# Two mixture-of-experts layers cut into runs of four token tiles in place of eight, each run with its own slots, buffers and conditional part

## The chip, the core and the metric

The kernel runs on one core of a Trainium2 chip. A core has five engines that each take instructions in order from a queue of their own: TensorE (PE, with the loading of its weights shown apart as PEld), VectorE (DVE), ScalarE (ACT), GpSimd (POOL) and SyncE (SP), which here only starts transfers. Sixteen DMA engines move data between the chip's memory (HBM) and the core's on-chip memory. The metric is the time of one execution in microseconds (us) on the device. Beside the times there is a trace of one profiled execution.

## The reference

The input x is 2 batches of 1024 tokens with 256 features, in 32-bit floats. Six steps add to it:

```python
x = x + 0.5 * L0_ffn(layernorm(x))      # 8 experts, each token goes to 2, hidden size 176
x = x + rwkv(layernorm(x))              # time mixing and channel mixing along each batch
x = x + 0.5 * L0_ffn(layernorm(x))
x = x + 0.5 * L1_ffn(layernorm(x))      # 32 experts, each token goes to 6, hidden size 96
x = x + L1_attn(layernorm(x))
x = x + 0.5 * L1_ffn(layernorm(x))
```

Only the last three are touched here. A layer of the second kind is

```python
scores = sigmoid(x @ gate_w)
topk_w, topk_i = top_k(scores, 6)
topk_w = topk_w / (sum(topk_w) + 1e-20)
combine = sum(one_hot(topk_i, 32) * topk_w[..., None], axis=1)
act = silu(einsum('td,edf->tef', x, wg)) * einsum('td,edf->tef', x, wu)
routed = einsum('tef,efd,te->td', act, wd, combine)
shared = silu(x @ sg) * (x @ su) @ sd
return routed + shared
```

The attention between the two is linear and sums over a whole batch: with Q, K and V from one product, `A = sum(feature_map(rope(K)) * V)` over the 1024 tokens of the batch, and the result is `(A * rope(Q)) @ W_out + b_out`, added to its input. So a batch can't leave the attention before all of its tokens have come through the first L1 mixture, while the two batches don't depend on each other.

## The kernel before, in words

x stays on the chip as 16 tiles of 128 tokens by 256 features. Tiles 0 to 7 are the first batch (called half A), 8 to 15 the second (half B). Four tiles are a group (`BT` is 4).

**A mixture** (`sparse_moe`, from line 400) computes only the experts that a token has chosen. Its parts are functions that a program outside of them calls piece by piece:

- `prep` normalizes a group's four tiles, transposes them and computes the router's scores; `plan` turns the choices into slot numbers, such that the tokens of one expert lie together and every expert starts at a multiple of 128.
- `scatter` (line 560) writes each token's row to the memory tile `xs`, once per chosen expert, at its slot: 24 indirect DMA calls on POOL for four tiles with six choices. Calls come in threes, with five short POOL memsets behind each three as a pause.
- `owners` works out which expert owns each block of 128 slots (the tile `who`) and how many blocks are in use (`used`). `weights` looks up the weight of each choice, on DVE.
- `blocks` (line 877) goes through the blocks. Each is fetched from `xs` by SP (`fetch`), transposed on PE (`features`, tile px), multiplied by its expert's gate and up matrices (`inner`, tile pg, with the expert's number in a PE register that `look_up` loads four at a time), gated on ACT and DVE, transposed again (`turn`, tile ph), multiplied by the down matrix (`outward`, tile py), copied by DVE to a tile yb and stored by SP to the memory tile `ys`. `step` issues one stage each of five neighbouring blocks, so they overlap.
- `shared` computes the shared expert of tiles; `combine` fetches each token's rows back from `ys` (24 indirect DMA calls on POOL, line 801, eight buffers yk) and adds them to x with their weights on DVE (line 813).

How many blocks are needed depends on the choices. Eight tiles with six choices and 32 experts can need up to 79 blocks (`moe_blocks`, each expert rounded up to a multiple of 128). The first 68 (`SURE`) are always computed. The other 11 stand in a conditional part: `tc.If(n > sure)` around `rest()` (line 906), where PE, DVE, ACT and SP each compare the count, loaded from `used` at block 16, and jump over the part where it is not needed. Blocks between the count in use and 68 hold zeros: `fill_slots` writes zeros to all of `xs`, and to the rows of `ys` that only the conditional part would write, ahead of the layers.

**The halves.** In each pass of an L1 mixture half A is a run of 68 blocks, then half B is one. The tiles are called L1_0A and L1_0B in the first pass, and L1_1A and L1_1B in the second. A half's first group of tokens may be gathered once 55 blocks are stored (a count that its four tiles can't exceed), the second group once all are.

**The order of the work** is written down when the program is built. The main program calls the blocks, and a planner (`clock`) with estimated durations (1.41 us for an L1 block, 4.8 us for a shared tile, 1.27 us for an indirect call, 1.4 us for a pause) lets other threads put in their instructions when they are due: scatters, gathers, the attention of a half with the preparation of its second mixture (`second_pass`). `settle` holds the main program until something is planned. On the chip each engine follows this order, and waits are for data and buffers alone. The main program before, in its last part: shared experts of 0A; blocks 0A with the attention's first steps due behind them; blocks 0B, with attention of A, its second preparation and 0B's shared tiles put between; then `settle(lambda: 1 in ready2[0])`, `shared_of(m2[0])` (all eight shared tiles of 1A) and `settle(lambda: 1 in sent2[0])`; blocks 1A; blocks 1B with its shared tiles as `part`; and behind them the gathers of 1B. From 0B's blocks to 1A's blocks no run is under way; the attention of batch B lies there.

The functions that the change touches, as they are before it:

## Time and profile before

| | |
|---|---|
| median of 8 runs | 1457.09 us (1455.04 to 1461.97) |
| the profiled execution | 1457.8 us, of which the trace's span is 1456.0 us |
| mean granted TensorE clock | 0.896 of full speed |
| PE busy | 1265.4 us, 87% of the span |
| weight loads (PEld) | 970.5 us, 67% |
| DVE busy | 736.0 us, 51% |
| POOL busy | 666.4 us, 46% |
| ACT busy | 622.8 us, 43% |
| moved by DMA | 214.94 MB, a mean of 148 GB/s |
| instructions | 23152 |

A busy time is the sum of an engine's instructions over the span, so PE's 87% is a mean over stages that differ. The L1 part takes the second half: the first L1 gate product is at 735.8 us, 0A's blocks run to about 850, 0B's to 1053, 1A's from 1168 to 1280, 1B's to 1397, and the program ends at 1456. In rows of groups the form is line, engine, operation, output<-input by the program's names, and the count behind an x; tiles of the second half of the first pass have 0B in their name. The granted clock tells how fast PE was let run: at 0.5 a product takes twice its time.

### The profile page before, as it was taken

To read this page: it belongs to the slowest core of one execution; us is meant where nothing else is said; L and a number is where in the kernel's file an instruction comes from. 1 tells how busy PE (TensorE), PEld (TensorE's weight loads), DVE (VectorE), ACT (ScalarE), POOL (GpSimd) and SP (SyncE) were. 2 spreads that over 40 slices of the span, in tenths; PEclk is the share of its full clock that TensorE was granted. 3 is DMA by queue.
4 is the path that set the end of the run, shared out by engine and by line. 5 is a ranking of instruction groups with operands and counts; after the bars stand their busy time and mean duration, and the time that the engine had idled before them with its cause. 6 is when DMAs were issued, how large, how long until landed. Compare 5 with 4: busy or idle time off the path is not lost. (4 is left out here: it accounts for less than half of the span.)

```text
span 1456.0 us, 23152 instructions
## 1 busy us (share of the span) xinstructions
PE 1265.4 (87%) x6100; PEld 970.5 (67%) x6100; DVE 736.0 (51%) x2507; ACT 622.8 (43%) x1671; POOL 666.4 (46%) x1346
## 2 busy tenths in 40 slices
PE   6699889889999789999889988988888789989970
PEld 4577657455666767766668977767655678978850
DVE  5333545855642432456354446764687354455553
ACT  4023553477664123442434545443323244544520
POOL 1630522001110640467777255505667777166465
PEclk9589889889999679989969999997789699999995
DMA  9723422980002723433757776533322267677743
GB/s 284 231 78 104 137 77 89 310 298 1 0 0 64 197 80 101 138 102 113 216 166 241 214 204 198 161 106 97 110 59 76 80 196 244 201 230 238 233 125 105
DMA packets 195170, 214.94 MB, mean 148 GB/s; under 512 B 40892, under 2 KB 178012, under 8 KB 195036
## 3 DMA queue, kind: packets, MB, share of 16 engines
q1 hardware_dynamic: 170460, 146.22, 32.6%
q0 software_dynamic: 24576, 67.14, 15.1%
q8 instruction: 59, 0.97, 0.3%
q14 instruction: 75, 0.61, 0.2%
HBM read 103.04 MB, written 110.23 MB: 146 GB/s over the span
## 5 line engine op out<-in xcount | busy, mean ns | idle before, releaser
L801 POOL DMA_INDIRECT yk_L<-ys_L,idx_L x64 | 62.1, 970 | 186.9 <-DMA ys_L<-yb_L 124.5
L333 POOL MEMSET still<- 128x96 f32 x628 | 112.5, 179 | 35.9
L764 PE MATMUL pg_L_b<-L0gu,xbT_L 128*128 x312 | 110.5, 479 | 0.0
L566 POOL DMA_INDIRECT xs_L<-xn_L,idx_L x64 | 61.9, 967 | 74.5 <-DVE idx_L L557 37.0
L659 PE MATMUL pg_L<-L0sgu,xTs_L 128*128 128x352 f32 x256 | 89.6, 484 | 2.9 <-DVE h_L L650 2.9
L801 POOL DMA_INDIRECT yk_L_0B<-ys_B,idx_L_0B x48 | 48.9, 1019 | 74.8 <-DMA ys_B<-yb_L_0B 46.8
L781 PE MATMUL py_L_b<-L0down,hT_L_b 88*128 x312 | 82.0, 385 | 0.0
L801 POOL DMA_INDIRECT yk_L_0A<-ys_A,idx_L_0A x48 | 46.3, 964 | 70.1 <-DMA ys_A<-yb_L_0A 31.9
L801 POOL DMA_INDIRECT yk_L_1A<-ys_A,idx_L_1A x48 | 46.1, 961 | 60.5 <-DMA xb_L_1A<-xs_A 29.1
L781 PEld LDWEIGHTS py_L_b<-L0down,hT_L_b 88*128 88x128 f32 x312 | 59.7, 194 | 20.0 <-issue 1.0
L764 PEld LDWEIGHTS pg_L_b<-L0gu,xbT_L 128*128 128x128 f32 x312 | 56.5, 198 | 20.1 <-issue 3.0
L650 DVE TENSOR_TENSOR h_L_b<-g_L_b,pg_L_b 128x176 f32<-128x176 f32 x78 | 26.2, 336 | 83.2 <-ACT g_L_b L649 73.4
L983 PE MATMUL pkk_cm<-mk_cm,w_WkeyT 128*128 128x512 f32 x128 | 62.7, 622 | 5.2 <-DVE mk_cm L975 3.5
L659 PEld LDWEIGHTS pg_L<-L0sgu,xTs_L 128*128 128x128 f32 x256 | 47.9, 199 | 25.6 <-DVE h_L L650 4.6
L764 PE MATMUL pg_L_0B_b<-L1gu,xbT_L_0B 128*128 x272 | 59.9, 346 | 1.2 <-DVEq L906 1.0
L764 PE MATMUL pg_L_0A_b<-L1gu,xbT_L_0A 128*128 x272 | 59.5, 344 | 1.6 <-ACT g_L_0A_b L649 0.7
L801 POOL DMA_INDIRECT yk_L_1B<-ys_B,idx_L_1B x48 | 45.7, 951 | 31.3 <-DMA xb_L_1B<-xs_B 13.4
L764 PE MATMUL pg_L_1B_b<-L1gu,xbT_L_1B 128*128 x272 | 56.5, 330 | 2.8 <-issue 1.3
L995 PE MATMUL pkv_cm<-w_WvalT,sk_cm 128*128 128x256 f32 x256 | 58.0, 379 | 0.1
L764 PE MATMUL pg_L_1A_b<-L1gu,xbT_L_1A 128*128 x272 | 57.6, 335 | 0.3 <-DVE m_L_1B L193 0.2
L995 PEld LDWEIGHTS pkv_cm<-w_WvalT,sk_cm 128*128 128x128 f32 x256 | 48.3, 190 | 12.0 <-issue 5.0
L649 ACT ACTIVATE g_L_b<-pg_L_b 128x176 f32<-128x176 f32 x78 | 24.7, 317 | 73.2 <-PE pg_L_b L764 61.5
(639 smaller groups left out, 3394.0 us busy)
## 6 DMA issues: line engine op xcount, KB each, us to landing
xs_A<-zero SPq DMA_DIRECT2D x1, 10112.0 KB
xs_B<-zero SPq DMA_DIRECT2D x1, 10112.0 KB
xb_L<-xs_L SPq DMA_DIRECT2D x78, 128.0 KB
ys_L<-yb_L SPq DMA_DIRECT2D x78, 128.0 KB
xb_L_0A<-xs_A SPq DMA_DIRECT2D x68, 128.0 KB
ys_A<-yb_L_0A SPq DMA_DIRECT2D x68, 128.0 KB
xb_L_0B<-xs_B SPq DMA_DIRECT2D x68, 128.0 KB
ys_B<-yb_L_0B SPq DMA_DIRECT2D x68, 128.0 KB
```

The costliest lines, as they stand in the source:

```text
L333: d = nc.gpsimd.memset(still, 0.0)
L566: d = nc.gpsimd.indirect_dma_start(out=xs, out_offset=bass.IndirectOffsetOnAxis(ap=idx[:, t, k : k + 1], axis=0), in_=sent[g][t - BT * g], ...
L649: nc.scalar.activation(g, pg[:, 0:width], AF.Silu)
L650: nc.vector.tensor_tensor(dst, g, pg[:, width : 2 * width], ALU.mult)
L659: nc.tensor.matmul(pg, xbT[:, c, i * P : (i + 1) * P], w["sgu"][:, c, u, :, :].rearrange("p z w -> p (z w)"), start=(c == 0), stop=(c == D ...
L764: nc.tensor.matmul(pg, xbT[:, c, :], w["gu"][:, c, bass.ds(e, 1), :, :].rearrange("p e z h -> p (e z h)"), start=(c == 0), stop=(c == DC - 1),
L781: mm = nc.tensor.matmul(py, hT[0:HP, k, :], w["down"][:, bass.ds(e, 1), k, :].rearrange("p e d -> p (e d)"), start=(k == 0), stop=(k == C ...
L801: d = nc.gpsimd.indirect_dma_start(out=yk, out_offset=None, in_=ys[0 : n * P, :], in_offset=bass.IndirectOffsetOnAxis(ap=idx[:, t, k : k + ...
L983: nc.tensor.matmul(ps, w[:, c, oc * P : (oc + 1) * P], src[:, c, :], start=(c == 0), stop=(c == DC - 1),)
L995: nc.tensor.matmul(ps, src[:, c, i * P : (i + 1) * P], w[:, c, :], start=(c == 0), stop=(c == n - 1),)
```

## The change

The L1 mixtures are cut by groups of four tiles. In each pass there are four runs instead of two, called 0A0, 0A1, 0B0, 0B1 and 1A0, 1A1, 1B0, 1B1. Each has

- its own memory tiles `xs[q]` and `ys[q]`, q from 0 to 3, of 55 blocks each instead of 79 for each half (the second pass uses the first one's again);
- 34 blocks that are always computed and 21 in a conditional part of its own, so that eight conditional parts stand in the program instead of four;
- its own plan, owners and weights; `who` and `used` have five buffers, `idx` and `wk` six. A mixture no longer has a second group, so all of its gathers wait for its conditional part.

The program around it follows: the first pass sends a group's tokens as soon as that group is planned; `run_of` puts the next run's first steps behind the last blocks of one, where the next one's scatters are planned by then. The attention of half A is due from 0A0 on, that of half B from 0B0's end on. In the first pass the shared tiles of half A stand ahead of 0A0 and those of half B beside and behind 0B1. In the second pass a run's shared tiles are put in a list (`left`) that `spare` deals from; `sent_or_fill` uses it where the main program would wait until a run's scatters are planned, and what is left over stands behind 1B1's blocks. The count of a run is loaded at its block 16, as before.

```diff
-SURE = {"L0": moe_blocks(MOE["L0"]), "L1": 68}
+SURE = {"L0": moe_blocks(MOE["L0"]), "L1": 34}
...
-    def sparse_moe(layer, w, name, x, xs, ys, moe, given=None, out=None, bufs=2):
+    def sparse_moe(layer, w, name, x, xs, ys, moe, given=None, at=0, out=None, bufs=2):
...
+        ahead = 5 if layer == "L1" else bufs
-        idx = back.tile([P, NT, K], I32, tag="idx", name=f"idx_{name}", bufs=3)
-        wk = back.tile([P, NT, K], F32, tag="wk", name=f"wk_{name}", bufs=2)
-        who = moe.tile([1, P], I32, tag="who", name=f"who_{name}", bufs=bufs)
-        used = moe.tile([1, 1], I32, tag="used", name=f"used_{name}", bufs=bufs)
+        idx = back.tile([P, NT, K], I32, tag="idx", name=f"idx_{name}", bufs=6)
+        wk = back.tile([P, NT, K], F32, tag="wk", name=f"wk_{name}", bufs=6)
+        who = moe.tile([1, P], I32, tag="who", name=f"who_{name}", bufs=ahead)
+        used = moe.tile([1, 1], I32, tag="used", name=f"used_{name}", bufs=ahead)
...
-            n = min(WHO, (sure if b < sure else NBLK) - b)
+            n = min(WHO - b % WHO, (sure if b < sure else NBLK) - b)
...
-    for k, layer, tiles in (("L0", "L0", NT), ("A", "L1", HT), ("B", "L1", HT)):
+    for k, layer, tiles in (("L0", "L0", NT), *((q, "L1", BT) for q in range(NB))):
...
-        for h in range(2):
-            fill_slots(xs["AB"[h]], moe_blocks(MOE["L1"], HT), behind=m["latest"]["add"])
+        for q in range(NB):
+            fill_slots(xs[q], moe_blocks(MOE["L1"], BT), behind=m["latest"]["add"])
             fill_slots(
-                ys["AB"[h]][SURE["L1"] * P :, :],
-                moe_blocks(MOE["L1"], HT) - SURE["L1"],
+                ys[q][SURE["L1"] * P :, :],
+                moe_blocks(MOE["L1"], BT) - SURE["L1"],
                 behind=m["latest"]["add"],
             )
...
+    def rows_of(m, qs, added, rank=0):
+        for g, q in enumerate(qs):
+            yield from wait(lambda: q in m and 0 in m[q]["ready"])
+            yield clock.now + 3.0
+            yield from m[q]["combine"](0, rank)
+            added.add(g)
...
+    def run_of(m, q, sent, part=None):
+
+        def beside():
+            if q + 1 < NB and q + 1 in sent:
+                return m[q + 1]
+            return pieces_of(part) if part is not None else None
+
+        all_of(m[q]["blocks"](beside))
...
-    shared_of(m1[0])
-    settle(lambda: 1 in sent1[0])
-    filled()
+    all_of(parts(m1[0], m1[1]))
+    settle(lambda: 0 in sent1)
     clock.begin(1, second_pass(0))
-    clock.begin(1, sends(m2, ready2, sent2, 0, 1))
-    all_of(m1[0]["blocks"](lambda: m1[1] if 1 in sent1[1] else None))
-    settle(lambda: 1 in sent1[1])
-    clock.begin(3, second_pass(1))
-    clock.begin(2, sends(m2, ready2, sent2, 1, 2))
-    part = m1[1]["shared"](0, HT)
-    all_of(m1[1]["blocks"](lambda: pieces_of(part)))
+    clock.begin(1, sends(m2, range(QS), ready2, sent2, 1))
+    for q in range(NB - 1):
+        run_of(m1, q, sent1)
+        settle(lambda: q + 1 in sent1)
+        if q == QS - 1:
+            clock.begin(3, second_pass(1))
+            clock.begin(2, sends(m2, range(QS, NB), ready2, sent2, 2))
+    part = parts(*(m1[q] for q in range(QS, NB)))
+    run_of(m1, NB - 1, sent1, part)
     all_of(part)
     summed.add(1)
-    settle(lambda: 1 in ready2[0])
-    shared_of(m2[0])
-    settle(lambda: 1 in sent2[0])
-    filled()
+
     done = [set(), set()]
-    clock.begin(4, given_rows(m2[0], range(2), done[0], 4))
-    all_of(m2[0]["blocks"](lambda: m2[1] if 1 in sent2[1] else None))
-    settle(lambda: 1 in sent2[1])
-
-    clock.begin(5, given_rows(m2[1], range(2), done[1], 5))
-    part = m2[1]["shared"](0, HT)
-    all_of(m2[1]["blocks"](lambda: pieces_of(part)))
+    for h in range(2):
+        clock.begin(4 + h, rows_of(m2, range(QS * h, QS * h + QS), done[h], 4 + h))
+    left = []
+
+    def spare():
+        while True:
+            us = None
+            while left and us is None:
+                us = next(left[0], None)
+                if us is None:
+                    left.pop(0)
+            yield us
+
+    part = spare()
+
+    def sent_or_fill(q):
+        while q not in sent2:
+            us = next(part)
+            clock.run(1.0 if us is None else us)
+
+    for q in range(NB):
+        while q not in ready2:
+            clock.run(1.0)
+        left.append(m2[q]["shared"](0, BT))
+        sent_or_fill(q)
+        run_of(m2, q, sent2, part)
     pauses["on"] = False
-    all_of(part)
+    all_of(iter(lambda: next(part), None))
     settle(lambda: 1 in done[0], lambda: 1 in done[1])
```

More of the change, by code (lines that the diff above doesn't have):

```diff
@@ L426, in places @@
         def places(t):
-            h, i = divmod(t, HT)
+            h, i = divmod(t + at, HT)
             if h not in xn:
@@ L622, in weights @@
         def weights(h):
-            ts = slice(HT * h, HT * h + HT)
+            n = min(HT, NT)
+            ts = slice(n * h, n * h + n)
             for k in range(K):
                 same = moe.tile(
-                    [P, HT, E], F32, tag="same", name=f"same_{name}_{h}_{k}", bufs=1
+                    [P, n, E], F32, tag="same", name=f"same_{name}_{h}_{k}", bufs=1
                 )
@@ L631, in weights @@
                     slot[:, ts, :],
-                    top[:, ts, k : k + 1].to_broadcast([P, HT, E]),
+                    top[:, ts, k : k + 1].to_broadcast([P, n, E]),
                     ALU.is_equal,
@@ L1392, in macaron_kernel, with quad_moe @@
     summed0 = {0}
-    added0, summed, ready1, ready2 = set(), {0}, [set(), set()], [set(), set()]
-    sent1, sent2 = [set(), set()], [set(), set()]
-    def half(n, h, **more):
-        k = "AB"[h]
-        return sparse_moe(
-            "L1", w1, f"L1_{n}{k}", x[HT * h : HT * h + HT], xs[k], ys[k], moe_pool, **more
+    added0, summed = set(), {0}
+    ready1, ready2, sent1, sent2 = set(), set(), set(), set()
+    QS = NB // 2
+    places_of = {}
+    def quad_moe(n, q, given, **more):
+        h, g = divmod(q, QS)
+        return sparse_moe(
+            "L1",
+            w1,
+            f"L1_{n}{'AB'[h]}{g}",
+            x[BT * q : BT * q + BT],
+            xs[q],
+            ys[q],
+            moe_pool,
+            given=given,
+            at=BT * g,
+            **more,
@@ L1400, in half, with onward @@
         )
-    def onward(m, g, planned):
+    def onward(m, q, planned):
         with behind_blocks():
-            m["prep"](g)
+            m["prep"](0)
         yield clock.spent(6.0, 12.0)
-        if g == 0:
-            yield from wait(lambda: not planning)
-            planning.append(m)
+        yield from wait(lambda: not planning)
+        planning.append(m)
         with behind_blocks():
-            m["plan"](g)
-        yield clock.spent(3.5, 7.0)
-        planned.add(g)
-        if g == m["groups"] - 1:
-            planning.pop()
@@ L1418, in first_pass @@
-    def first_pass(h):
-        for g in range(2):
-            yield from wait(lambda: 2 * h + g in added0)
-            if g == 0:
-                yield from wait(lambda: h in summed0)
-                m1[h] = half(0, h)
-            yield from onward(m1[h], g, ready1[h])
-        with behind_blocks():
-            m1[h]["owners"]()
-            m1[h]["weights"](0)
-        yield clock.now
+            m["plan"](0)
+        yield clock.spent(2.5, 5.0)
+        planned.add(q)
+        planning.pop()
@@ new lines, in onward @@
+        with behind_blocks():
+            m["owners"]()
+            m["weights"](0)
+        yield clock.now
+    def first_pass(h):
+        for q in range(QS * h, QS * h + QS):
+            yield from wait(lambda: q in added0 and h in summed0)
+            if q % QS == 0:
+                places_of[h] = (
+                    moe_pool.tile([P, HT, D], F32, tag="xn", name=f"xn_{h}", bufs=2),
+                    moe_pool.tile([P, DC, SEQ], F32, tag="xT", name=f"xTs_{h}", bufs=2),
+                )
+            m1[q] = quad_moe(0, q, places_of[h])
+            yield from onward(m1[q], q, ready1)
@@ L1431, in second_pass @@
     def second_pass(h):
         added, result = set(), {}
-        clock.begin(0, given_rows(m1[h], range(2), added))
+        qs = range(QS * h, QS * h + QS)
+        clock.begin(0, rows_of(m1, qs, added))
         yield from wait(lambda: h in summed)
         yield from attend(h, moe_pool, added, result)
-        m2[h] = half(
-            1,
-            h,
-            given=result["given"],
-            out=out[HT * h * P : (HT * h + HT) * P, :],
-        )
-        for g in range(2):
+        for q in qs:
+            m2[q] = quad_moe(
+                1, q, result["given"], out=out[BT * q * P : (BT * q + BT) * P, :]
+            )
@@ L1445, in second_pass @@
             with behind_blocks():
-                for t in range(BT * g, BT * g + BT):
+                for t in range(BT * (q % QS), BT * (q % QS) + BT):
                     result["out_of"](t)
             yield clock.spent(7.0, 8.0)
-            yield from onward(m2[h], g, ready2[h])
-        with behind_blocks():
-            m2[h]["owners"]()
-            m2[h]["weights"](0)
-        yield clock.now
-    def sends(m, planned, sent, h, rank):
-        for g in range(2):
-            yield from wait(lambda: g in planned[h])
-            yield from m[h]["scatter"](g, rank)
-            sent[h].add(g)
+            yield from onward(m2[q], q, ready2)
@@ L1462, in between, with sends @@
+    def rows_of(m, qs, added, rank=0):
[4 more added lines that the diff above has]
+            added.add(g)
+    def sends(m, qs, planned, sent, rank):
+        for q in qs:
+            yield from wait(lambda: q in planned)
+            yield from m[q]["scatter"](0, rank)
+            sent.add(q)
     def between():
         yield from given_rows(m0, (0, 1), added0)
-        yield from wait(lambda: 0 in ready1[0])
@@ L1465, in between @@
-        yield from m1[0]["scatter"](0)
+        yield from sends(m1, (0,), ready1, sent1, 0)
         yield from given_rows(m0, (2,), added0)
-        yield from wait(lambda: 1 in ready1[0])
-        yield from m1[0]["scatter"](1)
-        sent1[0].add(1)
+        yield from sends(m1, (1,), ready1, sent1, 0)
         yield from given_rows(m0, (3,), added0)
-        for g in range(2):
-            yield from wait(lambda: g in ready1[1])
-            yield from m1[1]["scatter"](g)
-        sent1[1].add(1)
+        yield from sends(m1, (2, 3), ready1, sent1, 0)
@@ L1476, in macaron_kernel, with parts @@
+    def run_of(m, q, sent, part=None):
[4 more added lines that the diff above has]
+        all_of(m[q]["blocks"](beside))
+    def parts(*ms):
+        for m in ms:
+            yield from m["shared"](0, BT)
     clock.begin(0, between())
@@ L1481, in macaron_kernel @@
     summed0.add(1)
-    settle(lambda: 1 in ready1[0])
+    settle(lambda: 1 in ready1)
     l0_stack.close()
```

## The prediction

> **What bounds the kernel now.** I read the stretches first (busy time of each engine between landmarks), then the rows of the block tiles, the engines' order of time around a conditional part, and last the gathers that end the program. In the stretches the columns after the length are busy us of PE, weight loads, DVE, ACT, POOL, then granted clock, DMA share and GB/s.

> ```profile
> core 0: us, PE busy (x) PEld busy (x) DVE busy (x) ACT busy (x) POOL busy (x), PEclk, DMA share, GB/s
> 735.00:850.00 115.00, 110.38 (x658) 96.43 (x657) 54.33 (x202) 56.71 (x207) 65.32 (x137) 0.93 0.67 208
> 850.00:1025.00 175.00, 152.64 (x786) 125.48 (x785) 103.77 (x327) 79.32 (x253) 79.26 (x169) 0.88 0.50 148
> 1025.00:1168.00 143.00, 118.27 (x481) 84.33 (x479) 90.93 (x322) 43.07 (x99) 103.22 (x209) 0.82 0.25 81
> 1168.00:1280.00 112.00, 108.25 (x666) 94.31 (x667) 51.13 (x191) 55.83 (x209) 65.84 (x138) 0.98 0.70 217
> 1280.00:1396.00 116.00, 109.16 (x645) 92.83 (x644) 64.14 (x196) 55.28 (x212) 65.13 (x138) 1.00 0.75 225
> 1396.00:1456.00 60.00, 15.19 (x59) 10.39 (x57) 25.34 (x57) 3.74 (x11) 37.19 (x44) 0.66 0.37 107
> ```

> PE bounds the runs (110 of 115, 108 of 112, 109 of 116 us). Two stretches are not PE's: 1025 to 1168, where no run is under way and the clock falls to 0.82, and the end, where PE does 15 of 60 us. The rows of the blocks' first transposition give the runs' length (duration min/median/max, first and last start):

> ```profile
> L742 PE MATMUL px_L_0A<-ident,xb_L_0A x136: 270/273/475, 734.0 to 848.6; 128*128 128x128 f32 x136
> ...
> L742 PE MATMUL px_L_0B<-ident,xb_L_0B x136: 270/273/473, 849.9 to 1024.3; 128*128 128x128 f32 x136
> ...
> L742 PE MATMUL px_L_1A<-ident,xb_L_1A x136: 270/273/477, 1168.3 to 1276.5; 128*128 128x128 f32 x136
> ...
> L742 PE MATMUL px_L_1B<-ident,xb_L_1B x136: 270/273/330, 1278.0 to 1384.7; 128*128 128x128 f32 x136
> ```

> Two transpositions make a block, so 1B passes 67 blocks in 106.7 us, and 1.52 us a block once 5 us for its start and its conditional are taken out. 0B takes 174.4 us for as many, since attention of batch A stands between its blocks. A conditional costs PE this (idle time and what ended it in brackets):

> ```profile
> 861.42 0.67 PE L781 MATMUL py_L_0B_b<-L1down,hT_L_0B_b 96*128 x2 [1.77 <-DVE yb_L_0A L789]
> 862.84 0.69 PE L742 MATMUL px_L_0B<-ident,xb_L_0B 128*128 128x128 f32 x2 [0.74 <-ACTq L906]
> 864.52 1.62 PE L764 MATMUL pg_L_0B_b<-L1gu,xbT_L_0B 128*128 x4 [1.00 <-DVEq L906]
> ```

> That is 3.5 us idle, and then matmuls of twice the length: between 864.4 and 869.4 the granted clock was 0.50, in the 5.4 us before 0.84. At 1A's conditional, 1286 to 1291, PE lost 1.8 us of 5 and the clock stayed 1.00. The last block's outputs leave DVE here, for 0B and for 1B:

> ```profile
> 1053.29 0.41 DVE L789 COPY yb_L_0B<-py_L_0B_b 128x256 f32<-128x256 f32 x1
> ...
> 1396.76 0.42 DVE L789 COPY yb_L_1B<-py_L_1B_b 128x256 f32<-128x256 f32 x1
> ```

> After 1396.8 come 44 of 1B's additions, one per gather, on one queue:

> ```profile
> L801 POOL DMA_INDIRECT yk_L_1B<-ys_B,idx_L_1B x48: 942/946/1069, 1379.8 to 1447.0; - x48
> L813 DVE SCALAR_TENSOR_TENSOR x<-yk_L_1B,wk_L_1B,x x48: 474/485/553, 1385.1 to 1449.8; 128x256 f32<-128x256 f32 x48
> ```

> **Blocks and conditionals.** Always-blocks stay 4 x 68 = 8 x 34 = 272, so the matmuls of blocks are the same. Counting the reference's choices on the given inputs, each group of 512 tokens needs 32 or 33 blocks, so no conditional part runs, before (68 fetches per run) or after. The skipped code is 21 blocks, not 11, and there are eight skips, not four. Four are new on PE's path: 0A0 (inside 0A1), 0B0 (inside 0B1), 1A0 and 1B0. Each I price at 5 us, between 3 (1A: 1.8 idle plus refilling) and 7 (0A: 3.5 idle plus half of some 6.8 us at half clock): +20, ends 12 and 28. Behind the skip wait DVE's copies, ACT's copies and SP's fetches, so PE sees all of it. A longer skip is in no row.

> [...]

> **The start, and what moves in the queues.** In the built order 0A0 needs only its own 24 scatters, but DVE's additions of L0's last gathers (POOL issues these at 719.6 to 733.5) and the copies of the turn tables still stand ahead of the first blocks' products, as before. So the first gate product stays at 736: 0, ends -8 and +3. On SP five to eight fetches of 0A0 now stand ahead of the loads of L1down; those waited on PE's py_L until 704.7 anyhow: 0. The zero fills grow from 180 to 304 blocks of 128 KB, 23.6 to 39.8 MB; the four fills now take 249.5 to about 325 us, each memset waiting on POOL for the fill before, so they would end near 377. The cover is DMA's idle stretch (327 to 436 us at 0 to 1 GB/s); POOL's adds of the channel mixes wait 0 to 3 us more. If that cover failed it would be +4.

> **The valley, step by step.** Before, 0B's last output is at 1053.3, with 4 of its 8 shared tiles done (2.4 us each: 1.45 pg, .38 ph and 1.03 py, overlapped). After, both preps of batch A's second mixture lie inside 0B1, as most of them did inside 0B, and the shared tiles follow: 1053.3 - 9.6 + 2 conditionals x 5 = 1053.7 for 0B1's last output. From there to the last block of 1B1:
> 8 shared tiles of 0B, 19.2; 0B1's conditional, 5 (before it stood in the valley); 136 blocks x 1.52 = 206.7; attention of batch B among 1A0's blocks; its remaining prep and out_of, 15 (pt 2.0, lg 3.7, po 4.1, ranks 3, a wait of 2 to 4); three conditionals, 15.
> Attention among blocks is read from 0B: 174.4 - 67 x 1.52 - 7 = 66 us above the blocks. It has no better row: its PE work alone is about 38, and the valley without shared tiles is 143 - 12 x 2.4 - 15 = 99; I take 66, the same work in the same setting. The sum is 1053.7 + 19.2 + 5 + 206.7 + 66 + 15 + 15 = 1380.6, against 1396.8. The 8 shared tiles of 1A, 19 us, are no longer on this way; they stand behind the blocks, under gathers. So filling the valley gains little: 34 blocks enter it, but attention's own waits for DVE and ACT come along.

> **POOL.** 24 calls with pauses take 38 us (each three 4.79). 0B1's gathers start at about 1070 and end at 1110; xs_1 ends by 1150; 1B0's indices are ready near 1180, so xs_2 ends at 1218 and xs_3 at 1257, before 1B0 and 1B1 fetch (1268, 1328). Three of 1B0's gathers stand ahead of 1A1's 24 in POOL's order: all 27 wait for 1B0's conditional at about 1328 and end at 1374, just under 1B1's blocks. If 1B1 were quicker, this would end last.

> **The end.** After the last output DVE has 49 additions instead of 44; none of these gathers has a pause. 59.2 + 5 x 1.3 - 2 = 64 us, ends 58 and 72. 12 shared tiles, 29 us, fit beside. Span 1380.6 + 64 = 1444.6. The profiled run took 1457.8 for a span of 1456.0, and the median of the eight is 0.7 below it, so the time is 1444.6 + 1.8 - 0.7 = 1446.

> **Rivals.**
> Forecast: as above, 1446 (its own range 1432 to 1458), chance 0.50: 0.40 faster, 0.06 same, 0.04 slower.
> Attention B hides: the blocks between fill its waits, 66 becomes 38, 1418. For it: clock 0.82 and POOL-bound gaps in the valley. Against: the same mixing in 0B left 152.6 busy of 175 at 0.88. 0.20, faster.
> The conditionals decide (slower): if each of the seven skips on the path costs 9 us, 5.4 lost and half of 6.8, 7 x 4 = 28 more, 1474. It turns slower when each costs 1.6 us above 5. For it: the half-clock row and the longer skip. Against: 1A's row. 0.20: 0.19 slower, 0.01 same.
> DVE or POOL sets the pace of 1A0: blocks 34 x 0.67, 24 additions x 0.48, attention 38, two preps 30, shared 3 make 105 of 145 us of DVE. If the queue order makes that end last, +16: 1462. 0.10: 0.09 slower, 0.01 same.

> **Numbers.** Blocks at 1.42 to 1.6 (-14, +11), attention 38 to 99 (-28, +33), conditionals -8 to +8 for the new four, end -6 to +8. Taken together rather than all at once, with the rivals: 1410 to 1476. A change under 0.2% (2.9 us) cannot be told from none. Faster 0.60, same 0.08, slower 0.32.

> **What would show it.** First gate product near 736; 0B1's last output near 1054; 1A0's blocks begun before 1085 and among attention B's; a clock near 1.0 from 1200 to the last block; last output near 1381, then 45 to 50 gathers at 1.25 us with shared products beside them. Wrong if idle time at the skips is well over 5 us, if PE waits on xb from xs_2 or xs_3, or if 1A0's blocks run far from 1.52 + 66/34.

## The result

| | before | after |
|---|---|---|
| median | 1456.78 us (46 runs, 1447.47 to 1464.44) | 1494.19 us (16 runs, 1485.16 to 1501.09) |
| profiled execution, span of the trace | 1457.8, 1456.0 us | 1497.06, 1494.5 us |
| mean granted clock | 0.896 | 0.882 |
| PE busy, moved by DMA | 1265.4 us, 214.94 MB | 1287.2 us, 231.47 MB |

The ratio is 1.0254, 95% interval [1.0235, 1.0272]: slower by 37 us, where 1446 us was forecast, 11 faster, and the range ended at 1476. The stretches of the changed kernel, with the columns of the prediction's first fence (length, busy us of PE, weight loads, DVE, ACT and POOL, clock, DMA share, GB/s):

```profile
735.00:850.00 115.00, 99.49 (x522) 83.08 (x523) 49.06 (x190) 46.83 (x164) 76.29 (x160) 0.85 0.60 189
850.00:1025.00 175.00, 149.11 (x797) 123.75 (x795) 108.65 (x323) 81.55 (x259) 82.16 (x169) 0.91 0.53 158
1025.00:1168.00 143.00, 126.07 (x604) 95.50 (x604) 91.35 (x328) 58.10 (x176) 91.70 (x187) 0.89 0.42 132
1168.00:1280.00 112.00, 95.89 (x524) 80.59 (x523) 53.79 (x226) 45.80 (x143) 59.08 (x122) 0.85 0.45 146
1280.00:1396.00 116.00, 105.86 (x616) 91.62 (x615) 56.99 (x170) 54.00 (x202) 54.96 (x114) 0.94 0.69 204
1396.00:1494.00 98.00, 58.83 (x223) 38.74 (x221) 44.51 (x112) 16.28 (x55) 54.63 (x69) 0.77 0.39 115
```

The valley, which lies between the run of 0B's blocks and that of 1A's in the kernel before, did fill (1025 to 1168 here): 604 products in place of 481, clock 0.89 for 0.82. The stretches on both sides lost it: 522 products for 658 from 735 to 850, 524 for 666 from 1168 to 1280, and an end that is 38 us longer with 44 us more of PE work in it. The landmarks are DVE's copies of an output block; these are the first of 0A0 and the last of 0A1, 0B1 and 1B1 in DVE's order of time:

```profile
766.77 0.42 DVE L791 COPY yb_L_0A<-py_L_0A_b 128x256 f32<-128x256 f32 x1 [0.79 <-PE py_L_0A_b L783]
...
879.73 0.43 DVE L791 COPY yb_L_0A<-py_L_0A_b 128x256 f32<-128x256 f32 x1
...
1083.12 0.42 DVE L791 COPY yb_L_0B<-py_L_0B_b 128x256 f32<-128x256 f32 x1
...
1415.93 0.42 DVE L791 COPY yb_L_1B<-py_L_1B_b 128x256 f32<-128x256 f32 x1 [0.58 <-PE ph_L_1A L678]
```

Against the forecast's sum of 1444.6 the span is 49.9 us too long. By these landmarks: 29.8 of it stands before 0B1's last output (1083.5 against 1053.7), 6.0 between that and 1B1's last (332.9 against 326.9), and 14.1 behind it (78.1 against 64).

A skip looks like this on PE, at 1B0's conditional part (start, length, instruction, and in brackets the idle time before it):

```profile
1352.68 0.67 PE L783 MATMUL py_L_1B_b<-L1down,hT_L_1B_b 96*128 x2
1358.07 0.66 PE L744 MATMUL px_L_1B<-ident,xb_L_1B 128*128 128x128 f32 x2 [4.72 <-PEq L908]
1358.80 1.62 PE L766 MATMUL pg_L_1B_b<-L1gu,xbT_L_1B 128*128 x4
```

PE stands for 4.72 us at the branch (L908), and the four gate products behind it take 1.62 us, where the same four take 0.82 six us later: from 1358.0 to 1364.2 the granted clock was 0.50. The eight skips of this run left PE idle for 2.9 to 4.9 us each. Before, 0A's skip cost 3.5 us idle and a clock of 0.50 behind it, but 1A's only 1.8 at 1.00.

### The profile page after: what moved, and what is told of

Its sections match the earlier page's. It is cut to its first block, busy times and chain, and to the rows that moved or that the text cites. A ratio compares the mean times of both kernels' runs of the same rounds, so it can differ in the third digit from the quotient of the medians.

```text
span 1494.5 us, 23271 instructions
## 1 busy us (share of the span) xinstructions
PE 1287.2 (86%) x6076; PEld 980.5 (66%) x6076; DVE 747.9 (50%) x2575; ACT 629.4 (42%) x1673; POOL 664.6 (44%) x1325
## 2 busy tenths in 40 slices
DMA packets 211130, 231.47 MB, mean 155 GB/s; under 512 B 40956, under 2 KB 193948, under 8 KB 210972
## 5 line engine op out<-in xcount | busy, mean ns | idle before, releaser
L333 POOL MEMSET still<- 128x96 f32 x608 | 108.8, 179 | 34.7
L803 POOL DMA_INDIRECT yk_L_0A<-ys,idx_L_0A x48 | 47.0, 980 | 64.5 <-DVE x L815 38.7
L803 POOL DMA_INDIRECT yk_L_1A<-ys,idx_L_1A x48 | 46.2, 963 | 57.4 <-DVE x L815 32.3
L567 POOL DMA_INDIRECT xs<-axl_at,idx_L_1B x48 | 46.4, 967 | 53.8 <-DVE same_L_1B L631 41.8
L652 DVE TENSOR_TENSOR h_L_b<-g_L_b,pg_L_b 128x176 f32<-128x176 f32 x78 | 26.3, 337 | 87.4 <-ACT g_L_b L651 77.8
L803 POOL DMA_INDIRECT yk_L_0B<-ys,idx_L_0B x48 | 47.4, 987 | 50.7 <-DVE x L815 14.6
L803 POOL DMA_INDIRECT yk_L_1B<-ys,idx_L_1B x48 | 47.0, 979 | 35.2 <-DVE x L815 15.0
L567 POOL DMA_INDIRECT xs<-axl_at,idx_L_1A x48 | 47.1, 980 | 32.9 <-DVE idx_L_1A L558 21.0
L766 PE MATMUL pg_L_1A_b<-L1gu,xbT_L_1A 128*128 x272 | 60.7, 349 | 0.5 <-issue 0.4
```

The costliest lines, as they stand in the source:

```text
L333: d = nc.gpsimd.memset(still, 0.0)
L567: d = nc.gpsimd.indirect_dma_start(out=xs, out_offset=bass.IndirectOffsetOnAxis(ap=idx[:, t, k : k + 1], axis=0), in_=sent[g][t - BT * g], ...
L652: nc.vector.tensor_tensor(dst, g, pg[:, width : 2 * width], ALU.mult)
L766: nc.tensor.matmul(pg, xbT[:, c, :], w["gu"][:, c, bass.ds(e, 1), :, :].rearrange("p e z h -> p (e z h)"), start=(c == 0), stop=(c == DC - 1),
L803: d = nc.gpsimd.indirect_dma_start(out=yk, out_offset=None, in_=ys[0 : n * P, :], in_offset=bass.IndirectOffsetOnAxis(ap=idx[:, t, k : k + ...
```

## The experiments

They were made in six groups, each group and its runs of the kernel before on one chip. Between groups the ratios are compared, and "us" worked out of a difference of ratios is that difference times 1456.

### The skips

**Four of eight conditional parts left out, e1** (those of 0A0, 0B0, 1A0, 1B0, the four that the change adds):

```diff
-                with tc.If(n > sure):
-                    rest()
+                if name[-1] == "1":
+                    with tc.If(n > sure):
+                        rest()
```

> The changed kernel without the conditional parts of 0A0, 0B0, 1A0 and 1B0 (their blocks 34 to 54 and the loads of their counts are left out; no block of them is in use on these inputs). Theory: a skip costs PE about 4.3 us of idle time and 2 to 2.5 us of half clock behind it, 6.5 in all, and all four lie on the way to the end: 4 x 6.5 = 26 us less, 1468. Rival: the skips stand where PE would soon have waited for DVE or for POOL's gathers anyway, and the end is POOL's: 5 to 12 us less, 1482 to 1489.

Measured 1468.67 us, ratio 1.0092 [1.0057, 1.0127], so 0.0162 or 24 us less: 5.9 us for each skip, give or take 1.5 by the intervals. The theory of costly skips had 1468.

**All eight left out, e2.** As above, with no conditional part and no load of the count.

> The changed kernel without any of its eight conditional parts (blocks 34 to 54 of each run are left out). Theory: seven skips on the way at 6.5 us and 4 us of the last one's: 49 us less, 1445. Rival as for the run with four fewer: 10 to 24 us less, 1470 to 1484, with POOL's gathers ending last all the same.

1454.25 us, ratio 0.9986 [0.997, 1.0001]: 39 us less than the change, level with the kernel before. The eight skips together are worth more than the whole of the loss, and runs of four without them don't gain what was forecast.

**The kernel before without its four, e3.** The same edit there.

> The kernel before without its four conditional parts (blocks 68 to 78 of each half are left out). Theory: three skips on the way at 5 to 6 us, and 3 of the last one's: 18 to 21 us less, 1437. With the run without any, it tells what runs of four tiles are worth by themselves: the theory says 1445 against 1437, so nothing is gained even then. Rival (the runs of four do fill the valley and the skips alone spoil it): the changed kernel without conditionals is 15 us or more below this one.

1457.45 us, ratio 1.0019 [0.9989, 1.0049]. The theory missed by 20 us: leaving its skips out gained the kernel before nothing. In the profiled executions its blocks do end sooner on both sides of the valley (0B's last output at 1047.9 for 1053.7, and from 1A's first output to 1B's last 211.4 us for 216.4), but the valley between takes 8.3 us back: 1A's first output comes at 1183.3, against 1180.8 with the skips. PE meets 1A's first block earlier in its order and waits there for the scatters of 1A, which POOL issues one after the other; with the skips this wait is 3.81 us:

```profile
1158.78 0.69 PE L742 MATMUL px_L_1A<-ident,xb_L_1A 128*128 128x128 f32 x2 [9.73 <-DMA xb_L_1A<-xs_A]
```

The attention's last products (po), which all stood ahead of 1A's blocks before, now lie between the first transposition and the first output, 24.5 us in place of 12.5. So the valley that the change fills took back what the old skips cost, and four skips could cost nothing where eight cost 39 us. How much of that is POOL's scatters and how much the other order on PE was not separated.

**Conditional parts of one block in place of 21, e7.** Same branches, counts and jumps; the 20 blocks that the given inputs never need are gone from the code.

```diff
-            for b in range(sure, NBLK):
+            for b in range(sure, sure + 1):
```

> The changed kernel with eight conditional parts of one block each instead of 21 (blocks 35 to 54 are left out, the counts, branches and waits stay). Theory: a skip is dear because the code behind the part has to be fetched; over 8 PE instructions in place of 170 the idle time of 4.3 us per skip falls to 2 us or less, and 15 to 30 of the 40 us that the conditional parts cost are gone: 1465 to 1480. Rival: any skip is dear, since all of the engines have to come to their branch and start again: idle time at the skips stays over 3.5 us and the time within 5 us of 1494.

1461.07 us, ratio 1.0026 [1.0002, 1.0051], 33 us less. The larger part of the cost is neither the comparison nor the wait for the count, but goes with the length of what is jumped over. At 0A0's skip PE's order of time reads

```profile
824.86 0.67 PE L783 MATMUL py_L_0A_b<-L1down,hT_L_0A_b 96*128 x2 [0.78 <-DVE yb_L_0A L791]
826.00 0.41 PE L744 MATMUL px_L_0A<-ident,xb_L_0A 128*128 128x128 f32 x2 [0.47 <-PEq L908]
826.56 0.91 PE L766 MATMUL pg_L_0A_b<-L1gu,xbT_L_0A 128*128 x4
```

0.47 us idle instead of 3.92, and no half clock. The queues that carry instructions moved less as well. Before, after, and with parts of one block (packets, MB, share of 16 engines):

```profile
q8 instruction: 59, 0.97, 0.3%
q14 instruction: 75, 0.61, 0.2%
```

```profile
q8 instruction: 69, 1.13, 0.3%
q14 instruction: 89, 0.73, 0.2%
```

```profile
q8 instruction: 56, 0.92, 0.3%
q14 instruction: 72, 0.59, 0.1%
```

The change adds 10 and 14 packets, and short parts take 13 and 17 away. In the changed kernel's trace PE's own branch instruction (COMPARE_BRANCH, L908) takes 1.94 to 4.49 us at the eight skips, and in seven of them two to four packets of these queues move meanwhile; at 0A1's, the one of 1.94 us, none does. In the kernel before, over parts of 11 blocks, it takes 0.32 to 0.47 us; on ACT, DVE and SP it is 45 to 72 ns in both. But a shorter program has less code to move in any case, so that the stop is a wait for code isn't shown.

**Parts of seven blocks, e14.** `sure + 7` in the same line.

> The changed kernel with conditional parts of seven blocks (blocks 41 to 54 are left out). Parts of one block gave 1461, of 21 blocks 1494. Theory: a skip costs a fetch as soon as the code behind the part isn't at hand, a step and not a slope; seven blocks are past it on some of the engines and at some of the skips only, so 1468 to 1480 with idle times of under 1 us at some skips and over 3 at others. Rival one: cost grows evenly with the length, 1.6 us for each block of the part: 1471 with all skips alike at 2 us. Rival two: seven blocks are as good as one, 1461.

1464.09 us, ratio 1.0095 [1.0062, 1.0129]. With 1, 7 and 21 blocks the ratio goes 1.0026, 1.0095, 1.0254: 1.67 us a block between the first two, 1.65 between the last two, for eight skips together, or about 0.2 us per skip and block. Each of these points has an interval of some 3 to 5 us to either side, so an even slope fits (the first rival), but a step is not ruled out: by its ratio the time is 1471 beside the kernel before's 1456.78, which lies in the theory's range too. The idle times fit neither. PE stood for 0.45 to 1.18 us at a time at its skips here, nowhere over 3, and the brackets mostly name DVE's or ACT's queue at the branch, as if every engine jumped for itself and the last one counted. At 0A0's skip the clock was 0.50 behind two such stops all the same (825.8 to 831.3), and the four gate products took 1.62 us:

```profile
824.34 0.41 PE L744 MATMUL px_L_0A<-ident,xb_L_0A 128*128 128x128 f32 x2 [0.47 <-PEq L908]
825.84 1.62 PE L766 MATMUL pg_L_0A_b<-L1gu,xbT_L_0A 128*128 x4 [1.09 <-DVEq L908]
```

**A hint ahead of the branch, e9**, some six blocks early, that it will be taken, on PE, DVE, ACT and SP.

```diff
+                if q == sure - 2 and sure < NBLK:
+                    with ExitStack() as st:
+                        for ins in lately.values():
+                            st.enter_context(tc.issue_after(ins))
+                        tc.mark_branch_hint_location(f"skip_{name}", "LikelyTaken", ENGINES)
...
-                with tc.If(n > sure):
+                with tc.If(n > sure, label=f"skip_{name}"):
```

> The changed kernel, whole, with a branch hint ahead of each of the eight conditional parts, on PE, DVE, ACT and SP: some six blocks (9 us) before the branch each engine is told that it will be taken, so that the code behind the part can be fetched beforehand. Theory: the 4.3 us of a skip are the fetch of the code behind it; with it fetched beforehand the idle time falls below 1.5 us per skip, as with parts of one block, and the time to 1455 to 1465. Rival: the fetch is bought at the hint instead of the branch, or the hint comes to nothing: 1488 or more.

1476.92 us, ratio 1.0183 [1.0141, 1.0224]: 10 us of the 33, between what the theory and the rival expected. At 0A0's skip PE still stood 4.02 us, at the others 1.7 or less. Where the other 23 us stay was not found.

**The same hints in the kernel before, e12.**

> The kernel before, whole, with hints at its four conditional parts. Without the parts it was no faster (1457 against 1456), since 1A's blocks then waited the longer for POOL's scatters. Theory: hints give nothing here either, within 3 us of 1456. Rival: the time without the parts was the same only because the order of the work had changed with them: 8 us or more below 1456.

1452.34 us, ratio 1.0012 [0.9987, 1.0038]: nothing, as when its skips were taken away. Here the attention's last products stand ahead of 1A's blocks, as in the kernel before, so this doesn't hang on another order; but hints took only a part of a skip away above, so it is the weaker test.

### The start

The first output of 0A0 came at 767.2, 14.0 us later than before, where 0 was forecast. The tile of zeros has one buffer, so each of now eight fills waits, with POOL's memset, for the fill before it. The tile's rows, issues first, then the idle time ahead of the memsets:

```profile
L291 SPq DMA_DIRECT2D xs<-zero x4: 359/360/370, 249.7 to 348.5; - x4
L291 SPq DMA_DIRECT2D ys<-zero x4: 359/360/371, 272.6 to 371.5; - x4
...
  DMA xs<-zero: 57.3, 4
  DMA ys<-zero: 20.5, 3
```

POOL stood 77.8 us there, before 46.5, and every landmark behind it is late: the load of L1's down matrix at 714.3 for 704.7.

**One tile of zeros for all fills, e4** (every byte is still written):

```diff
-        zero = const.tile([P, D], F32, tag="zero", name=f"zero_{n}")
-        nc.gpsimd.memset(zero, 0.0)
+        if not zeros:
+            zeros.append(const.tile([P, D], F32, name="zero"))
+            nc.gpsimd.memset(zeros[0], 0.0)
+        zero = zeros[0]
```

> The changed kernel with one tile of zeros for all fills, so that POOL has one memset instead of nine, and no memset waits for the fill before it; the fills move as much. Theory: POOL's work of the channel mixing no longer stands behind the memsets, the loads of the L1 weights start near 462 us instead of 467.6, and 6 us of that reach the end: 1488. Rival (the fills' traffic itself is what delays): the loads stay near 467, and the time within 2 us of 1494.

1480.19 us, ratio 1.0172 [1.0143, 1.0201], 12 us less than the change, twice what the theory had; first output at 755.3. Nearly all of the lateness was POOL's waits between the fills, not their bytes.

**The same in the kernel before, e5.**

> The kernel before with one tile of zeros for all fills. In the changed kernel the same edit gave 14 us, of which 8 were there when the L1 weights are loaded. Here the memsets wait 46.5 us for fills instead of 77.8. Theory: POOL's part of the channel mixing comes 3 to 6 us earlier and 4 to 8 us reach the end, 1449 to 1453. Rival: only the fills past 325 us collide with the channel mixing, which this kernel doesn't have: within 2 us of 1456.

1456.8 us, ratio 1.0 [0.9976, 1.0023]: there, 46.5 us of such waits cost nothing.

**Both causes away, e8** (no conditional parts, one tile of zeros):

> The changed kernel with one tile of zeros and without any conditional part (blocks 34 to 54 left out): what runs of four tiles are worth where neither fills nor skips cost anything. Theory: the two costs lie one behind the other, so they add: 1454 - 14 = 1440. Rival: with both gone POOL's scatters and gathers set the end, and only 4 to 8 us of the 14 come through: 1446 to 1450.

1447.44 us, ratio 0.9935 [0.9911, 0.9959], in the rival's range. The two add up in part: 7 of the 12 us come through. Runs of four with neither cost gain 0.65%, about 9 us.

### The end

The forecast let 12 shared tiles lie free behind the last block. The rows of 1B's gathers and additions, and what POOL and DVE waited for around them:

```profile
L803 POOL DMA_INDIRECT yk_L_1B<-ys,idx_L_1B x48: 943/949/1190, 1358.5 to 1485.2; - x48
L815 DVE SCALAR_TENSOR_TENSOR x<-yk_L_1B,wk_L_1B,x x48: 474/485/543, 1376.9 to 1488.2; 128x256 f32<-128x256 f32 x48
...
  DVE x L815: 15.0, 11
  issue: 10.3, 32
  SPq L908: 8.3, 2
```

POOL's gathers wait for buffers that DVE's additions (L815) free; those stand in DVE's queue behind the sums of the shared tiles (L710), which come when PE, ACT and DVE have passed a shared tile on to each other.

**Shared tiles of 1A1, 1B0 and 1B1 left out, e6.**

> The changed kernel with the shared expert of 1A1, 1B0 and 1B1 left out (12 tiles, 29 us of PE, that stand in and behind 1B1's last blocks). Theory: behind the last output POOL's gathers are held by DVE, whose additions stand in order behind the shared tiles' products and sums; without them the 78 us from the last output to the end become 62 to 66, and the time 1479 to 1483. Rival (what the prediction said: the tiles fit beside the gathers at no cost): within 3 us of 1494.

1483.14 us, ratio 1.0176 [1.0139, 1.0213], 11 us less. From the last output to the end it is 65.9 us in place of 78.1: the forecast's 64, plus 2. So the number of additions was right, and the cover of the shared tiles wrong. Why they pass so slowly is open: 15.4 us of DVE's time in the changed kernel's end are waits ahead of four of these sums that the trace puts to nothing on the core (see the last section).

**Hints and one tile of zeros, e10**, and **the same without POOL's pauses from 1B1 on, e11:**

> The changed kernel, whole, with the hints and with one tile of zeros for all fills. Theory: what both give alone, less some of the 14 us that POOL takes back (7 of them came through without conditional parts): 1447 to 1454, 2 to 9 us below the kernel before. Rival: hints come to nothing, 1480 as with one tile of zeros alone.

1470.6 us, ratio 1.0141 [1.0103, 1.018]: the theory missed by 16 us or more, the rival by 9.

> As the run with hints and one tile of zeros, and POOL's pauses left out from 1B1 on, not only behind its blocks. Theory: 27 gathers beside 1B1's blocks have nine pauses of 1.3 us; without them some 9 gathers more are done before the last output, and the end comes 8 to 11 us earlier, less 2 to 4 us that 1B1's fetches lose to denser gathers: 5 us below the run with hints and one tile. Rival: the fetches of blocks lose what the gathers gain: within 2 us of it, or above.

1468.95 us, ratio 1.011 [1.0069, 1.0151]. The intervals overlap; nothing follows.

### A version without the costs

**The conditional part as a loop over one block's code, e13**, whole work, with POOL at the branch too, and one tile of zeros:

```diff
-            for b in range(sure, NBLK):
-                fetch(b)
...
+            with tc.For_i(sure, n_used["n"], 1, hint_engines=()) as b:
+                nc.sync.dma_start(out=own["xb"], in_=xs[bass.ds(b * P, P), :])
```

> The changed kernel with one tile of zeros, and with each conditional part as a loop over its blocks, from 34 to the count in use, so that the code of one block stands for 21 (POOL takes part in the branches now, since the loop's barriers need all engines; on these inputs no loop is entered). Theory: the part's length is what a skip costs, so the loop costs what a part of one block does, 0.26% above the kernel before, and one tile of zeros takes 7 to 14 us off that: 1446 to 1454, below the kernel before by 2 to 10 us. Rival: the branches of POOL hold its scatters and gathers, 8 times 1 to 2 us: 1458 to 1468.

1447.1 us, ratio 0.9982 [0.9963, 1.0001]: 40 us less than the change, and 28 less than the unrolled parts with the same one tile of zeros, by code that is shorter. Its last output is 24.4 us earlier than before (1372.8 for 1397.2), but 75.5 us follow it, so the span is only 8 less. Stretch from the last output to the end:

```profile
1373.00:1448.00 75.00, 38.87 (x131) 25.26 (x129) 31.94 (x76) 8.30 (x25) 42.00 (x44) 0.71 0.37 106
```

**Without POOL's pauses**, from 1A1's blocks on (e15), and from 1B1's on (e16):

```diff
     for q in range(NB):
...
         sent_or_fill(q)
+        if q == 1:
+            pauses["on"] = False
```

> As e13 (the whole work, one tile of zeros, the conditional part as a loop of one block's code), but POOL's pauses are off from 1A1's blocks on, where e13 has them until the last block. Theory (POOL's order sets the end: 75.5 us from the last output to the end in e13 for 49 additions and 43 gathers): some 30 pauses of 1.4 to 1.6 us fall away, the gathers of 1A1 and 1B0 end earlier, fewer of them lie behind the last output, and the end comes 5 to 15 us under e13, a median of 1432 to 1442, ratio to before 0.985 to 0.995. Rival (the pauses protect the fetches of blocks, so denser gathers hold PE): last output of 1B1 later by about what the tail gains, within 3 us of e13's 1447.

1400.45 us against 1428.29 of the kernel before on that chip, ratio 0.9815 [0.9791, 0.9839], lower than the theory had.

> As e15, but the pauses are off from 1B1's blocks on only. Theory (POOL's order sets the end): about half of e15's gain, 3 to 8 us under e13's 1447, ratio to before 0.990 to 0.997. Rival (the transfers or the additions on DVE set the end): 1445 to 1449, no different from e13.

1408.51 us, ratio 0.9866 [0.9843, 0.989], lower too. The gathers of 1A and 1B in the loop version with its pauses (e13) and without them from 1A1 on (e15):

```profile
L808 POOL DMA_INDIRECT yk_L_1A<-ys,idx_L_1A x48: 942/948/1189, 1253.6 to 1369.6; - x48
...
L808 POOL DMA_INDIRECT yk_L_1B<-ys,idx_L_1B x48: 940/946/1182, 1321.3 to 1439.1; - x48
```

```profile
L808 POOL DMA_INDIRECT yk_L_1A<-ys,idx_L_1A x48: 940/946/1187, 1226.6 to 1314.0; - x48
...
L808 POOL DMA_INDIRECT yk_L_1B<-ys,idx_L_1B x48: 940/946/1111, 1315.3 to 1384.8; - x48
```

1A's last gather falls 55.6 us earlier, and the time from the last output to the end falls from 75.5 to 41.5 us (54.8 in e16, the run without them from 1B1 on). Not all of this is the pauses'. At 1B's first output, where e16's program is still that of e13, e16 is 22.8 us ahead already (1244.8 for 1267.6), about what the kernel before gains on this chip, 21.7. Behind the last output e13 has 49 additions, e16 44 and e15 29; at 1.25 us from gather to gather these are 6 and 25 us of the 20.7 and 34. The rest goes with something else: in e13's end 16.3 us of DVE's time are waits that the trace puts to nothing on the core, the longest on ACT and the longest on DVE being

```profile
1425.02 0.37 ACT L690 COPY hT_L_1B<-ph_L_1B 96x256 f32<-96x256 f32 x1 [9.90 <-remote]
1434.08 0.42 DVE L715 SCALAR_TENSOR_TENSOR x<-py_L_1B,x 128x256 f32<-128x256 f32 x1 [10.62 <-remote]
```

and the traces of e15 and e16 have no such wait anywhere. So fewer gathers behind the last output did shorten the end; whether the pauses or the chip took the unexplained waits away was not tried. Over 1B's blocks in e15 (1250 to 1352) PE was busy 100.5 of 102 us at a clock of 1.00, so there the denser gathers did not hold the fetches; 1A's, from first to last output, took 183.8 us, for 176.2 in e16.

**Controls.** This chip ran the kernel before 1.5% quicker than the one of e13, so e13 was run once more (e17), and the pauses were taken from the kernel before too (e18):

> The kernel of e13 once more, as a control for e15 and e16, whose chip ran the kernel before faster than e13's did. If the gain of e15 and e16 is the pauses' alone, the ratio to before is that of e13, 0.996 to 1.000; if it is partly the chip, the ratio here may be 0.99.

1448.38 us, ratio 0.9977 [0.996, 0.9994], as the first time. But that was on a third chip, and e13 has no run on the quick one: how much of the step from 0.998 to 0.9815 belongs to that chip was not separated.

```diff
     clock.begin(4, given_rows(m2[0], range(2), done[0], 4))
+    pauses["on"] = False
```

> The kernel before, whole, with POOL's pauses off from the start of 1A's blocks on. Theory (the pauses were part of what set the end in runs of four alone, where every gather waits for its conditional and three scatters of 24 share the last 200 us with them): the gathers of 1A go earlier here, but those of 1B wait for its last block anyhow, so at most the few of 1A left behind it gain: 0 to -6 us, ratio 0.996 to 1.000. Rival (the pauses cost the kernel before as much): ratio 0.985 or less, and then the gain of e15 is not the runs' own.

1513.63 us, ratio 1.0435 [1.0409, 1.0461]. Both expectations missed. Here the 48 scatters of 1B, not gathers, go without pauses beside 1A's first blocks. The stretch from 1160 to 1250 in the kernel before and in this one:

```profile
1160.00:1250.00 90.00, 82.72 (x491) 70.15 (x491) 43.67 (x171) 40.06 (x147) 64.94 (x136) 0.94 0.67 214
```

```profile
1160.00:1250.00 90.00, 47.35 (x220) 36.74 (x221) 22.06 (x92) 20.29 (x62) 46.34 (x48) 0.67 0.38 128
```

Under half of the products, though POOL's last scatter comes at the same time (1242.1 for 1240.7), since it waits 22.6 us for the slots. PE stands where the copy of a block on ACT is late (8.39 and 8.01 us ahead of two transpositions), and ACT's own waits are put to no engine:

```profile
1193.34 0.25 ACT L649 ACTIVATE g_L_1A_b<-pg_L_1A_b 128x96 f32<-128x96 f32 x1 [11.31 <-remote]
```

So the kernel before lost by going without the pauses, and the loop version, on another chip, gained. Three things differ: scatters or gathers, the order that the planner writes with cheaper calls, and the chip. Scatters without pauses are not enough for it: in e15 some 25 of 1B's scatters go without pauses too, from 1197.4 on beside 1A1's blocks, and PE has 270 products in the 50 us from 1200, as dense as the 491 in 90 above. Which of the rest makes the difference was not tried apart.

## Why the prediction was wrong, step by step

- **Conditionals, the largest term.** "Each I price at 5 us, between 3 and 7", so +20 for the four that are new. By e1 and e2 it is 5.9 us for each of the four and 39 for all eight. The unit price was nearly right. What failed is the sum: it charged four skips, because the kernel before had four already, and took those as a cost that stays the same. Before, the four were worth nothing together (e3, and e12 agrees), since the valley behind the first two took back what they cost; in runs of four there is no such valley, and the eight cost 39, not 20. That each of the eight holds back the next run is a reading: the runs show the sums for four and for eight. "The skipped code is 21 blocks, not 11" stood in the text, but no price was put to it; e7 and e14 show that it is the larger part of the price: parts of one block cost some 6 us in all.
- **The rival "the conditionals decide"**, 1474, had mechanism and sign right, at chance 0.20. It was short by the start and the end, and named the wrong size: 9 us each on seven skips.
- **"The first gate product stays at 736: 0."** It came at 745.4, the first output 14.0 late. The fills were seen to wait on POOL for each other, and were put down as hidden in DMA's idle stretch, with +4 if not. The cover named was that of the transfers; what ran late was POOL itself. e4: 12 us.
- **0A.** From the first to the last output 113.0 us, against 108.1 before and 5 for 0A0's skip: right.
- **0B, "1053.3 - 9.6 + 2 conditionals x 5".** The 9.6 did not go: the gate products of four shared tiles of 0B and one of their sums still stand ahead of 0B1's last output (from 1071.9), as they did ahead of 0B's before. That leg was 15.5 us over, the 9.6 and 5.9 that no run assigns.
- **From 0B1 to the end of 1B1.** The 9.6 saved here by those tiles was used up by four shared tiles of 1A0, which stand among 1B1's last blocks (from 1404.9) and not behind them. From 0B1's last output to 1A0's, with attention of batch B among the blocks, it took 149 us, against some 147: the 66 us for attention above the blocks were right, and the rival that hides it fell. The later 102 blocks ran at 1.56 us, once three skips of 5 and the shared tiles are taken out, against 1.52.
- **POOL.** "All 27 wait for 1B0's conditional at about 1328 and end at 1374": they waited for it, until 1358.5, and ended at 1411.5, just under 1B1's last output, as the order said.
- **The end.** 49 additions, as forecast, but 78.1 us and not 64: "12 shared tiles, 29 us, fit beside" cost 12 (e6).

By the runs, 19 us more for skips, 12 for the start and 12 for the end make 43 of the 49.9. They are not quite additive (e8), so the rest is not assigned. The runs of four are worth about 9 us where the skips and the start are away and the shared tiles of the end are not (e8), not the 30 that the forecast's terms hold without skips.

## What to carry to other kernels

A jump over unrolled code cost more the longer the code was (eight jumps over 1, 7 and 21 blocks cost some 6, 16 and 39 us in all), and again where the clock dropped after the stop (to 0.50 for some 4 to 6 us): make the rarely used part a loop of one body before adding more such parts (28 us less here). A cost that a kernel carries today may be hidden by a stall which the change removes, so price what is already there once more, for the new schedule. Of a chain of transfers that share one buffer, look at the engine that issues the next, not at the bandwidth (12 us here); and a tail that is bound by one queue is not empty for other work that its additions stand behind (11 us here).

## What the runs showed of the hardware

```profile
1473.25 0.37 ACT L685 COPY hT_L_1B<-ph_L_1B 96x256 f32<-96x256 f32 x1 [10.88 <-remote]
```

  The same kind of wait stands in e18's slow stretch, 23.5 us of it ahead of ACT's gates from 1160 to 1250, and nowhere in e15 and e16, whose gathers go without pauses for longer. In the changed kernel no packets of the instruction queues lie at these places; the cause stays open.
- The kernel before took 1428.29 us on one chip and 1449.98 to 1457.57 on the others, so times of different groups can't be set side by side without it.
